# Expert second layer on one Trainium2 core: another order of its products, product 1 in two parts, expert 0's weights requested earlier

## Chip, core, metric

The kernel runs on one NeuronCore of a Trainium2 chip. The metric is the device time of one execution in microseconds (us). Before the change, three runs took 947.87 us in the median (946.37 to 949.05).

## What is computed

The input is x, 4 batches of 1024 tokens of 512 float32 values. A first, conditional linear layer picks one 512x512 matrix per batch; its result xc is routed: each token goes to the one of 8 experts with the largest router probability, at most 512 tokens an expert. Each expert is two matrix products with a ReLU between. The result, scaled with the probability, is added to x.

```python
xc = einsum('bsd,bdh->bsh', x, W[cat_ids]) + b[cat_ids][:, None, :]
probs = softmax(xc @ Wr)                      # (4096, 8)
eidx, p_tok = argmax(probs), max(probs)       # one expert a token
xe = xc[dispatch]                             # (8, 512, 512): each expert's tokens
h  = maximum(einsum('ecd,edf->ecf', xe, W1), 0.0)   # F = 2048
ye = einsum('ecf,efd->ecd', h, W2) * p_tok
y  = x + scatter_add(ye)
```

## The kernel before

All products are float32 and use a seven-product scheme for 2x2 blocks (Strassen's in Winograd's form): both factors are cut in four blocks, VectorE (DVE) forms sums of blocks, TensorE (PE) multiplies seven pairs, numbered 1 to 7, and the results are added up in PSUM banks and by DVE.

The span has two parts. The first some 146 us are the conditional layer and the routing; xc goes to DRAM in two halves of the columns (`xc0_dram`, `xc1_dram`), written by line 511. After that come the eight experts e = 0 to 7, some 98 us each.

An expert's first layer runs over NG = 4 groups g of the 2048 columns. `first_layer(e, g, k)` is product k of group g: 4 matmuls of 128x256 (line 743; the profile counts two records for each float32 matmul). ScalarE (ACT) copies banks out (L758) and applies the ReLU (L763, L770), DVE adds (L762), and after the last product of a group, number 3, `sums` (L160 to L163) forms the block sums of the group's h, which the second layer multiplies. The weights w1 come in three rotating buffers, so a load of w1 waits until PE has left the buffer.

The second layer contracts over all 2048 columns of h. `second_layer(e, k)` is product k for k in 1, 6, 5, 7: two row tiles `at` of 8 matmuls 128x256 each, 16 in all (L797). Products 1, 6 and 7 are accumulated one on top of the other in the same PSUM bank `yx`; product 5 has the bank `yy`. After each product DVE adds the bank, scaled by `table`, to the `residual` rows (`add`, L788): two adds after 1 and after 6, four after 5 and after 7. Since 6 accumulates on 1 and 7 on 6, a product must wait until the adds of the one under it have read the bank.

The other three products, 2, 4 and 3, are again cut in seven small products each: `inner_sums(e, k)` lets DVE make 8 sums (L160 to L163 on h, L167 to L170 on w2), in place over the blocks of a product that PE has finished, and `inner_product(e, k, q)` runs 4 matmuls of 128x128 (L848) and one or two adds of 128x128 (L788). The small products have the banks x (1, 6, 7, 4 on top of each other), y (5, 3) and z (2).

`transpose_rows(e + 1, c)` (L716) turns the next expert's row tiles c = 0 to 3 between the products; ACT copies them out and DVE forms their sums (L726 to L730). For e = 0, whose rows are gathered by GpSimd (POOL, L688, lines of `gather`) from `xc0_dram` and `xc1_dram`, the transposes stand between the first products, the two column halves apart.

`load_w2(e)` (L666) is four loads of 1 MB on SyncE's queue (SP), `sum_w2(e, part)` (L167 to L170, 128x1024) is DVE's block sums of half of them, `fetch(e)` gathers the residual rows and the next expert's rows, and line 899 copies x to the output in three pieces in expert 0.

The order on PE and SP is that of the program text (`manual_schedule`). On DVE, ACT and POOL a scheduler chooses it; `behind(f)` asks that f comes after the latest of the adds L762, and the adds `add` have high priority. SP works through its list in order: a load that waits holds back those after it.

Of the kernel before, what the change touches and what calls it, by code (L numbers as in the profile page):

```python
# [11 lines left out]
ALU = mybir.AluOpType  # L12
# [4 lines left out]
P = 128  # L17
# [5 lines left out]
def kernel(  # L23
# [14 lines left out]
    E, _, F = w1.shape  # L38
# [8 lines left out]
    SC = CAP // P  # L47
    HK = KC // 2
    HC = SC // 2
    HD = D // 2  # L50
# [22 lines left out]
    def behind(f, *at):  # L73

        with tc.issue_after(latest[0].ins):
            f(*at)
# [68 lines left out]
    BANK = {1: "x", 2: "z", 3: "y", 4: "x", 5: "y", 6: "x", 7: "x"}  # L145
    OPENS = (1, 2, 5)
    LAST = {"x": 4, "y": 3, "z": 2}
    banks = {}

    def bank(pool, key, k, shape, name, bufs):  # L150

        tag = BANK[k]
        if k in OPENS:
            at = "_".join(str(n) for n in key)
            banks[key, tag] = pool.tile(shape, F32, tag=tag, bufs=bufs, name=f"{name}{tag}_{at}")
        return banks[key, tag]

    def sums(eng, a11, a12, a21, a22, s1, s2, s4):

        eng.tensor_tensor(s1, a21, a22, ALU.add)  # L160
        eng.tensor_tensor(a21, a11, a21, ALU.subtract)
        eng.tensor_tensor(s2, s1, a11, ALU.subtract)  # L162
        eng.tensor_tensor(s4, a12, s2, ALU.subtract)  # L163

    def differences(eng, b11, b12, b21, b22, t1, t2, t4):

        eng.tensor_tensor(t1, b12, b11, ALU.subtract)  # L167
        eng.tensor_tensor(b12, b22, b12, ALU.subtract)
        eng.tensor_tensor(t2, b22, t1, ALU.subtract)
        eng.tensor_tensor(t4, b21, t2, ALU.subtract)  # L170

    w1s, w2s = {}, {}
# [12 lines left out]
    def sum_w1(e, g):  # L185
        sums(nc.vector, *(w1s[e, g][:, k, :, :] for k in range(7)))
# [469 lines left out]
    ps_p = ctx.enter_context(tc.tile_pool(name="ps_p", bufs=2, space=PSUM, reuse_waits="tile"))  # L656
# [3 lines left out]
    def load_w2(e):  # L660

        names = ("b11", "b12", "b21", "b22", "t1", "t2", "t4")
        t = {k: w2p.tile([P, NG * HB, D // 2], F32, tag=k, name=f"w2_{k}_{e}") for k in names}
        for k in ("b11", "b21", "b12", "b22"):
            i, j = int(k[1]) - 1, int(k[2]) - 1
            nc.sync.dma_start(  # L666
                out=t[k],
                in_=w2[
                    e, i * F // 2 : (i + 1) * F // 2, j * D // 2 : (j + 1) * D // 2
                ].rearrange("(m p) d -> p m d", p=P),  # L670
            )
        w2s[e] = t
# [64 lines left out]
    def first_layer(e, g, k):  # L737

        key = (1, e, g)
        ps = bank(ps_p, key, k, [P, HB, HC * P], "h", bufs=2)  # L740
        for j in range(HB):
            for kc in range(HK):
                nc.tensor.matmul(  # L743
                    ps[:, j, :],
                    lhsT=w1s[e, g][:, LEFT[k], kc, j * P : (j + 1) * P],
                    rhs=xes[e][:, RIGHT1[k], kc, :],
                    start=(k in OPENS and j == 0 and kc == 0),
                    stop=(k == LAST[BANK[k]] and j == HB - 1 and kc == HK - 1),
                    skip_group_check=True,
                )  # L750
        if e not in hs:
            hs[e] = hp.tile([P, NG, 7, HB, HC * P], F32, tag="h", name=f"h_{e}")
        h = hs[e][:, g, :, :, :]
        if k in (1, 6, 7):
            banks[key, k] = snap.tile(
                [P, HB, HC * P], F32, tag=f"s{k}", bufs=2, name=f"s{k}_{e}_{g}"
            )
            nc.scalar.copy(banks[key, k], ps)  # L758

        def total(into, ps, part):  # L760
            with tc.high_priority():
                latest[0] = nc.vector.tensor_tensor(into, ps, part, ALU.add)  # L762
            nc.scalar.activation(into, into, AF.Relu)  # L763

        if k == 2:
            total(h[:, 0, :, :], ps, banks.pop((key, 1)))
        if k == 7:
            total(h[:, 3, :, :], banks[key, "y"], banks.pop((key, 7)))
        if k == 4:
            nc.scalar.activation(h[:, 1, :, :], ps, AF.Relu)  # L770
        if k == 3:
            total(h[:, 2, :, :], ps, banks.pop((key, 6)))
            sums(nc.vector, *(h[:, i, :, :] for i in range(7)))
# [10 lines left out]
    def add(e, ps, half, at, columns):  # L784

        row = residual[e * SC + half * HC + at][:, columns]
        with tc.high_priority():
            nc.vector.scalar_tensor_tensor(  # L788
                row, ps, table[:, half * HC + at, e, 0:1], row, ALU.mult, ALU.add
            )  # L790

    def second_layer(e, k):

        ps = bank(ps_p, (2, e), k, [P, HC, HD], "y", bufs=2)
        for at in range(HC):
            for m in range(NG * HB):
                nc.tensor.matmul(  # L797
                    ps[:, at, :],
                    lhsT=hs[e][:, m // HB, LEFT[k], m % HB, at * P : (at + 1) * P],
                    rhs=w2s[e][RIGHT2[k]][:, m, :],  # L800
                    start=(k in OPENS and at == 0 and m == 0),
                    stop=(k in ENDS and at == HC - 1 and m == NG * HB - 1),
                    skip_group_check=True,
                )
        for half, part in {1: [(0, 0)], 6: [(0, 1)], 5: [(1, 1), (0, 1)], 7: [(1, 1), (1, 0)]}[k]:
            for at in range(HC):
                add(e, ps[:, at, :], half, at, slice(part * HD, (part + 1) * HD))
# [69 lines left out]
    def between(e, g):  # L877

        if g == 0 and e > 0:
            behind(sum_w1, e, W1G - 2)  # L880
        if g > 0:
            if e > 0 or g > 2:
                first_layer(e, g - 1, 4)
                first_layer(e, g - 1, 3)
            ahead = e * NG + g - 1 + W1G
            if ahead < E * NG:
                load_w1(*divmod(ahead, NG))
            if ahead > W1G and ahead <= E * NG:
                behind(sum_w1, *divmod(ahead - 1, NG))
        if g >= 2:  # L890
            behind(sum_w2, e, g - 2)
        if g == 1:
            behind(fetch, e)
        if e == 0 and g > 0:

            if g == 1:
                load_w2(0)
            q = slice((g - 1) * T // (NG - 1) // P * P, g * T // (NG - 1) // P * P)
            nc.sync.dma_start(out=of[q, :], in_=xf[q, :])

    with tc.manual_schedule(engines={mybir.EngineType.PE, mybir.EngineType.SP}):
        gather(0, xg, xc_dram, rows, src_row)

        for part, half, then in (
            ([0], 0, [(0, 1)]),
            ([0], 1, [(1, 1), (0, 5), (1, 5)]),
            ([1], 0, [(0, 2)]),
            ([1], 1, [(1, 2)]),
        ):
            for c in range(half * HC, (half + 1) * HC):  # L910
                transpose_rows(0, c, part)
            for g, k in then:
                first_layer(0, g, k)
        for e in range(E):
            for g in range(NG):
                if e == 0 and g < 2:

                    for k in ((6, 7), (4, 3))[g]:
                        first_layer(e, 0, k)
                        first_layer(e, 1, k)  # L920
                    between(e, g)
                    continue
                first_layer(e, g, 1)
                first_layer(e, g, 2)
                between(e, g)
                first_layer(e, g, 6)
                first_layer(e, g, 5)
                first_layer(e, g, 7)
            second_layer(e, 1)
            first_layer(e, NG - 1, 4)  # L930
            first_layer(e, NG - 1, 3)
            if (e + 1) * NG - 1 + W1G < E * NG:
                load_w1(e + 1, W1G - 1)
            inner_sums(e, 2)
            for c, k in enumerate((6, 5, 7)):
                second_layer(e, k)
                if k in (6, 5):
                    inner_sums(e, 4 if k == 6 else 3)
                if e + 1 < E:
                    transpose_rows(e + 1, c)  # L940

            TURNS = (1, 5, 2, 6, 3, 7, 4)
            for q in TURNS:
                if q == 4 and e + 1 < E:
                    transpose_rows(e + 1, SC - 1)
                inner_product(e, 2, q)
            for q in TURNS:
                inner_product(e, 3, q)
                inner_product(e, 4, q)
            if e + 1 < E:  # L950
                load_w2(e + 1)

# [30 lines left out]
```

## Time and profile before

| | |
|---|---|
| median of 3 runs | 947.87 us (946.37 to 949.05) |
| the profiled execution | 947.93 us, span 946.1 us |
| mean granted TensorE clock | 0.996 |
| PE busy | 923.4 us, 98% of the span |
| DVE busy | 617.7 us, 65% |
| ACT, POOL busy | 185.6 us and 177.9 us, 20% and 19% |
| DMA | 123.28 MB, mean 130 GB/s |

Times in the views count from the start of the span. A row of a timeline gives the start, the length, the engine, the source line, the operation, the tiles it writes and reads, the shape, the number of records and, in brackets, how long the engine was idle before it and what ended that. The modelled end of a matmul lies some 0.16 us after the start of the next one, so a gap of PE in brackets is by that much shorter than the time that its issue lost.

### The profile page before, as it was taken

The page shows a single profiled execution, that of the slowest core. Times are in us where ns is not written, and L with a number is a line of the kernel's source. Part 1 is how long each engine was busy: PE and PEld are TensorE (multiplying, and loading weights), DVE is VectorE, ACT ScalarE, POOL GpSimd, SP SyncE. Part 2 cuts the span into 40 slices and gives each one's busy share as a digit, 9 for nine tenths or more (in the row PEclk, how much of TensorE's full clock was granted, in tenths as well). Part 3 has the DMA queues.
Part 4 walks back from the last instruction along what each step waited for, and adds up shares of the span by engine and source line. Part 5 has one row for each costly group of instructions (what it writes and reads, how often), then busy time and mean ns, then how long its engine had stood idle before and what let it go on. Part 6 is the DMA issues. An engine that isn't in the chain of part 4 may idle for free.

```text
span 946.1 us, 12760 instructions
## 1 busy us (share of the span) xinstructions
PE 923.4 (98%) x5126; PEld 814.6 (86%) x5126; DVE 617.7 (65%) x1134; ACT 185.6 (20%) x317; POOL 177.9 (19%) x173
## 2 busy tenths in 40 slices
PE   9999999989999999999999999999999999999996
PEld 6788787878988898889888998899889988998886
DVE  4656673578449844985478647963797468745782
ACT  3333201310132103210330023101310132013200
POOL 0042342230141013200230024001500150012001
PEclk9999999999999999999999999999999999999999
DMA  9474223695633153314441345115520652062001
GB/s 307 158 233 155 84 91 94 211 387 202 222 116 107 45 190 128 129 45 148 137 155 45 103 163 171 54 52 171 178 89 5 216 177 89 1 219 89 0 1 45
DMA packets 95724, 123.28 MB, mean 130 GB/s; under 512 B 8516, under 2 KB 83268, under 8 KB 95474
## 3 DMA queue, kind: packets, MB, share of 16 engines
q1 hardware_dynamic: 85634, 97.54, 30.8%
q0 software_dynamic: 9216, 24.85, 8.0%
q8 instruction: 40, 0.66, 0.3%
q14 instruction: 18, 0.15, 0.1%
q10 hardware_dynamic: 816, 0.08, 0.1%
HBM read 105.96 MB, written 25.23 MB: 139 GB/s over the span
## 4 chain that ended last, share of the span: by engine, by line
PE 74%; issue 17%; DVE 4%; POOL 2%; DMA 2%; ACT 1%; SPq 1%; POOLq 0%; DVEq 0%
PE hx L743 18%; PE yx L797 11%; PE hy L743 8%; PE yx L848 7%; PE xcx_lin L488 6%; PE hz L743 4%; PE yy L797 4%; PE yy L848 3%; PE xcy_lin L488 2%; PE yz L848 2%; DMA w_b<-in_L_ffn_W_dram 2%; PE xcz_lin L488 1%; PE ps_xT L273 1%; PE ps_e L716 1%; POOL rows L688 1%
## 5 line engine op out<-in xcount | busy, mean ns | idle before, releaser
L743 PE MATMUL hx<-xe,w 128*128 128x256 f32 x1024 | 237.7, 379 | 1.2 <-DVE xe L717 1.0
L743 PEld LDWEIGHTS hx<-xe,w 128*128 128x128 f32 x1024 | 193.8, 190 | 27.7 <-DVE xe L717 1.2
L867 POOL DMA_INDIRECT out_dram<-rows,dst_row x32 | 32.0, 999 | 496.8 <-DVE rows L788 492.2
L743 PE MATMUL hy<-xe,w 128*128 128x256 f32 x512 | 120.6, 379 | 0.0
L797 PE MATMUL yx<-w_b,h 128*128 128x256 f32 x512 | 113.1, 379 | 0.0
L743 PEld LDWEIGHTS hy<-xe,w 128*128 128x128 f32 x512 | 97.3, 190 | 13.2
L797 PEld LDWEIGHTS yx<-w_b,h 128*128 128x128 f32 x512 | 96.7, 190 | 12.9
L758 ACT COPY s<-hx 128x512 f32<-128x512 f32 x96 | 55.8, 581 | 240.8 <-PE hx L743 240.8
L788 DVE SCALAR_TENSOR_TENSOR rows<-yx,table,rows 128x128 f32<-128x128 f32 (+1 forms) x160 | 60.0, 400 | 60.1 <-PE yx L848 37.1
L762 DVE TENSOR_TENSOR h<-hy,s 128x512 f32<-128x512 f32 x64 | 44.0, 688 | 74.6 <-PE hy L743 50.2
L763 ACT ACTIVATE h<-h 128x512 f32<-128x512 f32 x96 | 60.5, 630 | 159.5 <-DVE h L762 159.5
L797 PE MATMUL yx<-w_t,h 128*128 128x256 f32 x256 | 60.5, 391 | 10.6 <-DVE h L162 8.7
L688 POOL DMA_INDIRECT rows<-in_x_dram,at x32 | 41.2, 1288 | 139.6 <-DVE at L699 106.2
L797 PEld LDWEIGHTS yx<-w_t,h 128*128 128x128 f32 x256 | 49.1, 194 | 20.8 <-DVE h L162 11.9
L688 POOL DMA_INDIRECT rows<-xc_dram,at x56 | 58.6, 1047 | 17.1 <-issue 15.2
L743 PE MATMUL hz<-xe,w 128*128 128x256 f32 x256 | 60.6, 379 | 0.6 <-DVE xe L717 0.6
L762 DVE TENSOR_TENSOR h<-hz,s 128x512 f32<-128x512 f32 x32 | 22.0, 688 | 57.5 <-PE hz L743 57.5
L797 PE MATMUL yy<-w_t,h 128*128 128x256 f32 x256 | 56.6, 379 | 0.0
L743 PEld LDWEIGHTS hz<-xe,w 128*128 128x128 f32 x256 | 48.5, 190 | 7.4 <-DVE xe L717 0.9
L460 POOL DMA_INDIRECT slots<-row,dest x32 | 36.3, 1135 | 95.8 <-DVE dest L456 87.3
L797 PEld LDWEIGHTS yy<-w_t,h 128*128 128x128 f32 x256 | 48.1, 190 | 6.2
L717 ACT COPY xe<-ps_e 128x512 f32<-128x512 f32 x28 | 16.4, 586 | 182.9 <-PE ps_e L716 182.9
(154 smaller groups left out, 1258.4 us busy)
## 6 DMA issues: line engine op xcount, KB each, us to landing
w<-in_L_ffn_W_dram SPq DMA_DIRECT2D x64, 512.0 KB, 4.2
w_b<-in_L_ffn_W_dram SPq DMA_DIRECT2D x32, 1024.0 KB, 6.9
x<-in_x_dram SPq DMA_DIRECT2D x7, 1024.0 KB, 8.6
xc_dram<-s SPq DMA_DIRECT2D x22, 256.0 KB, 2.7
out_dram<-in_x_dram SPq DMA_DIRECT2D x2, 2816.0 KB, 23.9
cw<-in_L_cond_W_dram SPq DMA_DIRECT2D x3, 1024.0 KB, 9.9
out_dram<-in_x_dram SPq DMA_DIRECT2D x1, 2560.0 KB, 18.9
xc_dram<-xc SPq DMA_DIRECT2D x8, 256.0 KB, 2.3
```

Of the source, the lines that this page charges most:

```text
L460: nc.gpsimd.indirect_dma_start(out=slots, out_offset=bass.IndirectOffsetOnAxis(ap=dest[:, j : j + 1], axis=0), in_=row[:, j, :], in_offset ...
L488: nc.tensor.matmul(ps[:, j, :], lhsT=left[:, kc, j * P : (j + 1) * P], rhs=right[k][:, kc, :], start=((k in OPENS or (b, k) == (LATE, 3)) ...
L688: nc.gpsimd.indirect_dma_start(out=into[e * SC + c][:, j * n : (j + 1) * n], out_offset=None, in_=source, in_offset=bass.IndirectOffsetOnA ...
L717: (nc.vector.tensor_copy if e == 0 else nc.scalar.copy)(t[:, 2 * half + parts[0] : 2 * half + parts[0] + n, :, at * P : (at + 1) * P].rear ...
L743: nc.tensor.matmul(ps[:, j, :], lhsT=w1s[e, g][:, LEFT[k], kc, j * P : (j + 1) * P], rhs=xes[e][:, RIGHT1[k], kc, :], start=(k in OPENS an ...
L758: nc.scalar.copy(banks[key, k], ps)
L762: latest[0] = nc.vector.tensor_tensor(into, ps, part, ALU.add)
L763: nc.scalar.activation(into, into, AF.Relu)
L788: nc.vector.scalar_tensor_tensor(row, ps, table[:, half * HC + at, e, 0:1], row, ALU.mult, ALU.add)
L797: nc.tensor.matmul(ps[:, at, :], lhsT=hs[e][:, m // HB, LEFT[k], m % HB, at * P : (at + 1) * P], rhs=w2s[e][RIGHT2[k]][:, m, :], start=(k ...
L848: nc.tensor.matmul(ps, lhsT=left[:, g, :], rhs=right[:, g, :], start=(q in OPENS and g == 0), stop=(q == LAST[BANK[q]] and g == NG - 1), s ...
L867: nc.gpsimd.indirect_dma_start(out=of, out_offset=bass.IndirectOffsetOnAxis(ap=dst_row[:, n : n + 1], axis=0), in_=residual.pop(n), in_off ...
```

## The change

In words: product 1 of the second layer is issued in two halves, one row tile before the last two first-layer products (4 and 3 of group 3) and one after them; then come products 5, 6 and 7, where before it was 6, 5, 7. The sums for the small products follow their new order (product 3's after 5, product 4's after 6). The small products take other turns: number 4 of group 2 stands behind the next expert's last transpose and the first of group 3; then come pairs of 3 and 4 in another order. In `sums` and `differences` the second and third operation change places. Expert 0's w2 is requested right after the first small set of first-layer products in the program text, ahead of the load of w1 for group 3, and its sums are asked for one group earlier.

```diff
     def sums(eng, a11, a12, a21, a22, s1, s2, s4):
         eng.tensor_tensor(s1, a21, a22, ALU.add)
+        eng.tensor_tensor(s2, s1, a11, ALU.subtract)
         eng.tensor_tensor(a21, a11, a21, ALU.subtract)
-        eng.tensor_tensor(s2, s1, a11, ALU.subtract)
         eng.tensor_tensor(s4, a12, s2, ALU.subtract)
     # differences: t2 before b12, in the same way
...
-    def second_layer(e, k):
-        ps = bank(ps_p, (2, e), k, [P, HC, HD], "y", bufs=2)
-        for at in range(HC):
+    def second_layer(e, k, tiles=range(HC)):
+        if tiles[0] == 0:
+            bank(ps_p, (2, e), k, [P, HC, HD], "y", bufs=2)
+        ps = banks[(2, e), BANK[k]]
+        for at in tiles:
...
+        if tiles[-1] < HC - 1:
+            return
...
-        if g >= 2:
-            behind(sum_w2, e, g - 2)
+        part = g - 2 + (e == 0)
+        if part in (0, 1):
+            behind(sum_w2, e, part)
...
-            if g == 1:
-                load_w2(0)
...
+        behind(load_w2, 0)          # ahead of the loop over the experts
...
-            second_layer(e, 1)
+            second_layer(e, 1, [0])
             first_layer(e, NG - 1, 4)
             first_layer(e, NG - 1, 3)
+            second_layer(e, 1, [1])
...
             inner_sums(e, 2)
-            for c, k in enumerate((6, 5, 7)):
+            for c, k in enumerate((5, 6, 7)):
                 second_layer(e, k)
-                if k in (6, 5):
-                    inner_sums(e, 4 if k == 6 else 3)
+                if k in (5, 6):
+                    inner_sums(e, 3 if k == 5 else 4)
                 if e + 1 < E:
                     transpose_rows(e + 1, c)
-            TURNS = (1, 5, 2, 6, 3, 7, 4)
-            for q in TURNS:
-                if q == 4 and e + 1 < E:
-                    transpose_rows(e + 1, SC - 1)
+            for q in (1, 5, 2, 6, 3, 7):
                 inner_product(e, 2, q)
-            for q in TURNS:
-                inner_product(e, 3, q)
-                inner_product(e, 4, q)
+            if e + 1 < E:
+                transpose_rows(e + 1, SC - 1)
+            for k, q in (
+                *[(3, 1), (2, 4), (3, 5)],
+                *[(4, 1), (4, 5), (3, 2), (4, 2), (3, 6), (4, 6)],
+                *[(3, 3), (4, 3), (3, 7), (4, 7), (3, 4), (4, 4)],
+            ):
+                inner_product(e, k, q)
```

More of the change, by code (lines that the diff above doesn't have):

```diff
@@ L167, in differences @@
         eng.tensor_tensor(t1, b12, b11, ALU.subtract)
+        eng.tensor_tensor(t2, b22, t1, ALU.subtract)
         eng.tensor_tensor(b12, b22, b12, ALU.subtract)
-        eng.tensor_tensor(t2, b22, t1, ALU.subtract)
         eng.tensor_tensor(t4, b21, t2, ALU.subtract)
```

## The prediction, made before the changed kernel was run

> **What bounds the kernel.** I read the page's first part and the waits of PE first, then the timelines of one expert's second layer.
>
> ```profile
> PE 923.4 (98%) x5126; PEld 814.6 (86%) x5126; DVE 617.7 (65%) x1134; ACT 185.6 (20%) x317; POOL 177.9 (19%) x173
> ```
>
> TensorE is busy all the time and the change neither adds nor removes a matmul. So only PE's idle time, and stretches at a lower clock, can move. The list of who waited for whom, PE alone, says where they are:
>
> ```profile
> PE yx L797 <- DVE h L162: 8.7, 8, 2.4
> PE yx L797 <- DVE rows L788: 1.8, 1, 1.8
> PE yx L848 <- DVE rows L788: 0.4, 1, 0.4
> ```
>
> Once in each expert, product 6 waits for the sum L162 (s2 of the last group's h), and in expert 0 it waits before that for the adds of product 1. The PE timelines of expert 0 and expert 1:
>
> ```profile
> 204.44 1.89 PE L743 MATMUL hy<-xe,w 128*128 128x256 f32 x8
> 208.16 2.86 PE L797 MATMUL yx<-w_t,h 128*128 128x256 f32 x12 [1.83 <-DVE rows L788]
> 213.40 6.27 PE L797 MATMUL yx<-w_t,h 128*128 128x256 f32 x20 [2.38 <-DVE h L162]
> 219.51 0.60 PE L716 MATMUL ps_e<-ident,rows 128*128 128x128 f32 x4
> ...
> 309.36 2.75 PE L797 MATMUL yx<-w_t,h 128*128 128x256 f32 x12
> 313.03 4.58 PE L797 MATMUL yx<-w_t,h 128*128 128x256 f32 x20 [0.91 <-DVE h L162]
> 317.45 0.60 PE L716 MATMUL ps_e<-ident,rows 128*128 128x128 f32 x4
> 317.88 7.07 PE L797 MATMUL yy<-w_t,h 128*128 128x256 f32 x32
> ```
>
> A product of 16 matmuls takes 6.91 us when nothing waits (317.88 to the next transposes at 324.79), 0.432 us a matmul. In expert 1 product 6 is issued from 309.36 to 317.45, so 1.18 us are lost: the wait and 0.1 us of slow start. In expert 0 it could start at 206.17 and ends at 219.51, so 6.43 us are lost. The two waits don't explain that: 20 records took 6.27 us, not 4.58. The table by stretches does; the third number from the end is the granted clock, which is 1.00 in the stretches before and after:
>
> ```profile
> 214.00:218.00 4.00, 4.00 (x13) 3.21 (x11) 4.00 (x7) 0.00 (x0) 0.00 (x0) 0.57 1.15 448
> ```
>
> After 4.2 us of idleness within 7 us the clock was halved for a while, which cost 1.64 us. All eight losses add up to 6.43 + 7 x 1.18 = 14.7 us.
>
> **The new order: what goes.** Product 5 needs s1 only, and half of product 1 (3.46 us) now stands behind the last first-layer product. In expert 1's times: half of 1 at 299.00, the products 4 and 3 from 302.46 to 305.91, the other half to 309.36, then 5. The sum s1 comes at about 308.2 and is needed at 5's seventh matmul, at 311.95. So the 14.7 us go.
>
> **What comes.** Product 7 accumulates on product 6, and they are now neighbours, with only the transposes (0.43 us) between. In the changed instruction order 7's first matmul waits for the second of 6's two adds, both of which wait for 6's last matmul. Before, product 5 (6.91 us) lay between. And the adds stand in DVE's list behind all sums that the new order packs there. DVE's spacings are in its timeline of expert 1:
>
> ```profile
> 309.56 0.69 DVE L762 TENSOR_TENSOR h<-hy,s 128x512 f32<-128x512 f32 x1 [0.48 <-PE hy L743]
> 310.95 0.69 DVE L160 TENSOR_TENSOR h<-h 128x512 f32<-128x512 f32 x1 [0.69 <-ACT h L763]
> 311.68 0.69 DVE L161 TENSOR_TENSOR h<-h 128x512 f32<-128x512 f32 x1
> 312.29 0.68 DVE L162 TENSOR_TENSOR h<-h 128x512 f32<-128x512 f32 x1
> ...
> 317.83 0.87 DVE L788 SCALAR_TENSOR_TENSOR rows<-yx,table,rows 128x256 f32<-128x256 f32 x2
> 318.62 0.68 DVE L163 TENSOR_TENSOR h<-h 128x512 f32<-128x512 f32 x1
> ```
>
> L762 to L160 is 1.39 us (the ReLU between), a sum 0.60 us, 0.73 us when it needs the one before it, two adds 0.79 us, four 1.57 us. From the end of first-layer product 3 (306.09 now) the list runs without a gap: 1.39; four sums 2.53; adds of product 1 0.79; eight sums 4.82; two sums 1.21; four adds of 5 1.57; six sums 3.62; four sums 2.54; two adds of 6 with the signal 0.92. That ends at 325.48, while PE could start 7 at 324.05: 1.43 us and a slow start of 0.10. I take 1.53 us for experts 0 to 6. In expert 7 there are no transposes and the adds stand one sum earlier: 324.88 against 323.19, so 1.79 us. Sum 12.5 us. The net of this part is **-2.2 us**: expert 0 wins 4.9, the other seven lose 2.7. It holds for expert 0 because its DVE no longer lags: it stood idle for w_b's DMA 2.1 and 3.4 us there, and the w2 sums now come before 195 us.
>
> **The turns of small products.** Small product 4 of group 2 waits for the add of 7 today. Behind the transposes the issue starts 0.17 us late and loses 0.10 more, seven times; in expert 7, without transposes, 0.71 us: 2.6 us in all. The order puts (3,1), 0.89 us, between, and this goes. But (4,1) reuses the bank of (2,4), whose add ends just when (4,1) could start (2.67 against 2.68 us after the transposes, by the same rows): between 0 and 0.27 us each; I take 0.1, near a slow start alone. **-1.9 us** (-2.6 to -0.7).
>
> **Expert 0's weights.** The four loads have nothing left to wait for when SP reaches them: they follow the last write of xc, issued at 147.51 us, while before the load of w1 ahead of them held them until 174.6. At the 308 to 373 GB/s of the stretches from 176 to 190 us the 4 MB are under way for 11 to 14 us, from 148 to about 162, when POOL gathers expert 0's rows. The DMA view of 140 to 225 us shows what a gather takes from issue to landing in three conditions: expert 0's own (2.7 us for the four of the second half, which have the queues to themselves), those with copies of x in flight, and those with w2 in flight.
>
> ```profile
> rows<-xc_dram,src_row POOLq DMA_INDIRECT x8, 2.9
> rows<-xc_dram,at POOLq DMA_INDIRECT x8, 10.0
> rows<-in_x_dram,at POOLq DMA_INDIRECT x4, 6.0
> ```
>
> The second tile of the second half is issued at 151.80 and lands at 154.5; PE wants it at 155.86 and hides up to 1.36 us of delay. At 6.0 us it lands at 157.8: PE waits **+2.0 us**; the third and fourth tile are hidden by that. Bounds: nothing (gathers beside one 1 MB load of w1 had medians of 2.7 to 3.4), and 5.9 us at 10.0. The third row is the nearest: pieces of w2 in flight and hardly a copy yet. A wait of 2.0 beside the 0.63 us already there may halve the clock; 1.6 more. The Trainium skill, "DMA: Bandwidth & Descriptors" (Queues, rings and completion order), says that each DMA engine takes packets from its queues in turn. By that rule a small gather would lose only an equal share, this term would be near nothing and the sum 943.8. The Trainium skill, "TensorE: Matmul & The Clock Gate" (Part 1), ties a halved clock to an idle window of about 3.4 us; by it no wait here would halve it, though in the trace gaps of 1.83 and 2.38 us did.
>
> **What costs nothing.** The exchanged lines in `sums` bring s2 0.6 us earlier. The load of w1 for group 3 is now behind w2 on SP, but waits until 173.5 for its buffer anyway, after the queue is empty; if not, PE needs it at 183.7, five us after it landed before. The index copy for `fetch` slips some 6 us behind the w2 sums on DVE, and POOL's twelve gathers with it; expert 1's first tile, landed at about 203 before, lands at 209 and is needed at 213. The next w2 loads start about 1 us later, long before DVE wants them.
>
> **Sum.** Against the profiled 947.93 us (the median is 947.87): -2.2 - 1.9 + 2.0 gives **945.8 us**. A measurement of this kernel can tell about 0.3%, 2.8 us, from no change: faster means under 945.0, slower over 950.7.
>
> **Rivals.**
> 1. The gathers aren't delayed by more than 1.4 us: 943.8, own range 942.8 to 944.6. For it: the rows beside w1. Against: those loads were 1 MB, this stream is 4 MB. Chance 0.25.
> 2. Slower: the gathers take the 10 us of the second row, PE stands 5.9 us at 156 and restarts at half clock, 1.64: 947.93 - 4.1 + 7.6 = 951.4. It decides from about 9 us of landing. Against: that row had copies in flight. Chance 0.14, with 0.03 for halved clocks at the eight new waits (up to 13 us; the seven of 0.91 us left it whole).
> 3. The change does all it says and product 7 finds its adds done: 947.93 - 14.7 - 1.9 + 2.0 = 933.3. Against: the adds can't start before product 6 ends, and take longer than the transposes. Chance 0.05.
>
> The likeliest case has 0.53 and its own range is 944.0 to 947.6 (DVE's list 0.2 us longer or shorter in each expert, the bounds of the small products, 1 to 3.6 us for the gathers); 0.06 of it is under 945.0. Faster: 0.25 + 0.05 + 0.06 = 0.36. Slower: 0.14 + 0.03 = 0.17. The range of 8 in 10 leaves out rival 3 and the far ends of the others: 943.0 to 951.0.
>
> **What would show it.** Right: in the waits of PE, L799 on DVE h L162 is gone, and L799 on DVE rows L788 stands there eight times, with about 1.25 us each and 1.5 in expert 7; a new wait at L716 for gathered rows near 156 us; the clock stays whole at 214. Wrong: product 7 starting right behind the transposes, a wait of product 5, or gathers of 2.7 us near 150.

## The result and the profile after

The changed kernel takes 949.16 us in the median of 18 runs (947.78 to 950.89), the kernel before 946.85 in 18 runs beside it: 1.0023 times as long, 95% interval 1.0016 to 1.0030. Two later groups of runs gave 1.0010 (0.9995 to 1.0024) and 1.0017 (1.0008 to 1.0027). The forecast was 2.1 us less than before; it became some 2 us more. The profiled execution took 949.79 us, its span is 948.0.

The page's busy times, then two rows from the list of who waited for whom, PE alone (us in total, times, longest):

```profile
PE 922.8 (97%) x5126; PEld 815.7 (86%) x5126; DVE 612.6 (65%) x1134; ACT 185.5 (20%) x317; POOL 185.8 (20%) x173
```

```profile
PE yx L799 <- DVE rows L788: 10.6, 8, 1.6
PE ps_e L716 <- DMA rows<-xc_dram,src_row: 2.3, 2, 1.7
```

The row "DVE h L162" is gone. Its place is taken by eight waits at product 7, and two waits for gathered rows are new. The PE timeline of expert 1 shows one of the eight:

```profile
317.10 7.07 PE L799 MATMUL yx<-w_t,h 128*128 128x256 f32 x32
324.01 0.60 PE L716 MATMUL ps_e<-ident,rows 128*128 128x128 f32 x4
325.95 7.17 PE L799 MATMUL yx<-w_b,h 128*128 128x256 f32 x32 [1.33 <-DVE rows L788]
```

Product 7 could start 0.43 us after the transposes, at 324.44, and starts at 325.95: 1.51 us, and 0.10 more in its slow start. The start of expert 0, PE again:

```profile
153.41 3.62 PE L743 MATMUL hy<-xe,w 128*128 128x256 f32 x16
158.69 0.41 PE L716 MATMUL ps_e<-ident,rows 128*128 128x128 f32 x2 [1.66 <-DMA rows<-xc_dram,src_row]
159.74 0.41 PE L716 MATMUL ps_e<-ident,rows 128*128 128x128 f32 x2 [0.65 <-DMA rows<-xc_dram,src_row]
160.67 3.61 PE L743 MATMUL hz<-xe,w 128*128 128x256 f32 x8 [0.52 <-DVE xe L717]
```

In the profile of before, the same transposes and the same product hz follow one another without a wait for rows:

```profile
155.64 0.60 PE L716 MATMUL ps_e<-ident,rows 128*128 128x128 f32 x4
156.87 1.99 PE L743 MATMUL hz<-xe,w 128*128 128x256 f32 x8 [0.63 <-DVE xe L717]
```

That is 10.28 us after the first transposes (146.59), against 12.87 now (160.67 after 147.80). POOL had issued the two gathers that PE waits for here:

```profile
152.10 0.94 POOL L688 DMA_INDIRECT rows<-xc_dram,src_row  x1 [5.73 <-issue]
153.35 0.94 POOL L688 DMA_INDIRECT rows<-xc_dram,src_row  x1 [0.30 <-DVE xe L726]
```

They take 6.5 and 6.3 us from issue to landing, the third and fourth 5.7 and 5.6. The eight records of hz take 3.61 us; four records further on the same product of the other group takes 1.89. The table by stretches has the granted clock third from the end:

```profile
156.00:160.00 4.00, 1.69 (x9) 0.97 (x7) 0.42 (x1) 0.00 (x0) 0.79 (x1) 1.00 1.08 369
160.00:164.00 4.00, 3.48 (x10) 2.71 (x9) 0.42 (x1) 0.00 (x0) 0.00 (x0) 0.57 1.08 352
```

The clock is halved behind the waits. To place the loss I cut each profiled execution at PE's own marks: the first transposes of expert 0, its first second-layer matmul, the first matmul of expert 1 and of expert 7, the last matmul. Four profiles of before and three of the changed kernel (the later ones are among the experiments) give, in us:

| Profile | start | e0, first layer | e0, second layer | e1 to e6 | e7 |
|---|---|---|---|---|---|
| before | 146.59 | 49.22 | 58.30 | 587.61 | 96.50 |
| before_again | 146.92 | 49.95 | 54.75 | (590.42) | 96.51 |
| before_3 | 147.11 | 49.23 | 57.44 | 587.62 | 96.51 |
| before_4 | 148.07 | 49.23 | 57.82 | 587.62 | 96.51 |
| after | 147.80 | 53.41 | 53.29 | 589.12 | 96.49 |
| after_again | 146.84 | 54.75 | 53.83 | (591.67) | 96.49 |
| after_3 | 147.24 | 54.36 | 53.46 | 589.16 | 96.49 |

In brackets: profiles in which PE stood for some 0.2 to 1.6 us at a time at first-layer products, with nothing but its own issue behind it, now in one expert and now in another; 0.7 of the 49.95 is a stop too, which that profile puts down to ACT's copy (L758). The start is unchanged code and scatters by 1.5 us. The means differ by +4.8 in expert 0's first layer, -3.55 in its second, +1.5 in the six experts e1 to e6, and nothing in e7: +2.7 together, against 1.7 to 2.3 by the medians.

### The profile page after: what moved, and what is told of

Same layout as the page of the kernel before. It is cut to its first block, busy times and chain, and to the rows that moved or that the text cites. A ratio compares the mean times of both kernels' runs of the same rounds, so it can differ in the third digit from the quotient of the medians.

```text
span 948.0 us, 12759 instructions
## 1 busy us (share of the span) xinstructions
PE 922.8 (97%) x5126; PEld 815.7 (86%) x5126; DVE 612.6 (65%) x1134; ACT 185.5 (20%) x317; POOL 185.8 (20%) x173
## 4 chain that ended last, share of the span: by engine, by line
PE 44%; issue 26%; DVE 9%; POOL 3%; DMA 1%; ACT 0%; POOLq 0%; DVEq 0%
PE hx L743 16%; PE hy L743 7%; PE yx L852 6%; PE yx L799 6%; PE hz L743 4%; PE yy L852 3%; POOL rows L688 2%; DVE rows L788 2%; PE yz L852 1%; DVE h L161 1%; DVE h L160 1%; DVE h L163 1%; POOL out_dram L871 1%; DVE h L162 1%; DMA rows<-xc_dram,src_row 1%
## 5 line engine op out<-in xcount | busy, mean ns | idle before, releaser
L799 PE MATMUL yx<-w_b,h 128*128 128x256 f32 x512 | 115.3, 381 | 10.6 <-DVE rows L788 10.6
L758 ACT COPY s<-hx 128x512 f32<-128x512 f32 x96 | 55.8, 582 | 240.3 <-PE hx L743 240.3
L688 POOL DMA_INDIRECT rows<-in_x_dram,at x32 | 45.1, 1411 | 149.3 <-DVE at L699 106.3
L688 POOL DMA_INDIRECT rows<-xc_dram,at x56 | 62.6, 1119 | 20.4 <-issue 14.0
L799 PE MATMUL yx<-w_t,h 128*128 128x256 f32 x256 | 56.6, 379 | 0.0
```

The source lines that it names most:

```text
L688: nc.gpsimd.indirect_dma_start(out=into[e * SC + c][:, j * n : (j + 1) * n], out_offset=None, in_=source, in_offset=bass.IndirectOffsetOnA ...
L799: nc.tensor.matmul(ps[:, at, :], lhsT=hs[e][:, m // HB, LEFT[k], m % HB, at * P : (at + 1) * P], rhs=w2s[e][RIGHT2[k]][:, m, :], start=(k ...
```

## The experiments

Theory A: what the change does to the order behaves as forecast, and the loss against the forecast is expert 0's start, where the w2 loads delay the gathers. Rival B: the new order itself is the loss. Each kernel was timed beside the kernel before on the same chip; where the medians of two groups of runs differ, only the ratios to before are compared.

**1. Gathers first.**

```diff
+    landed = dram.tile([P, 1], F32, name="landed")
...
+        nc.sync.dma_start(out=landed, in_=rows[SC - 1][:, D - 1 : D])
         behind(load_w2, 0)
```

> The changed kernel, with a 512-byte copy of the last gathered row tile of expert 0 ahead of its w2 loads on SP, so that these four loads start only when all eight gathers have landed (some 156 us instead of 149). Theory A (the loss against the forecast sits in expert 0's start: the w2 loads delay the gathers, 4.2 us between the first transposes and product hy at 171.6 in the trace of before): this kernel is 4.2 us faster than the changed one, about 945.0 us, and some 2 us faster than before; no wait of PE at L716 for gathered rows, clock whole at 157 to 165 us, and the eight waits at product 7 stay. Rival B (the new order of products, not the loads, is the loss): within 1 us of the changed kernel, about 949. Rival C (the later loads bring back expert 0's waits for w2 sums at 208 to 218 us): some 945 + up to 5 = 950.

Measured: 945.09 us, 0.9965 of before (0.9952 to 0.9979); 49.22 us in expert 0's first layer. The time is A's 945.0. By the ratios to before (0.9965 against 1.0023) it is 5.5 us less than the changed kernel's, more than the 4.2 that A took from one profile; the three profiles of the changed kernel lie 4.2 to 5.5 us above 49.22, 4.95 in the mean. So the loss at the start goes, whole. The two kernels' answers on transfers (median us from issue to landing), the changed kernel's row first:

```profile
rows<-xc_dram,src_row POOLq DMA_INDIRECT x6, 5.6
```

```profile
rows<-xc_dram,src_row POOLq DMA_INDIRECT x5, 2.7
...
landed<-rows SPq DMA_DIRECT2D x1, 0.5 KB, 7.8
```

And PE has neither the wait nor the halved clock:

```profile
156.35 0.60 PE L717 MATMUL ps_e<-ident,rows 128*128 128x128 f32 x4
157.58 1.99 PE L744 MATMUL hz<-xe,w 128*128 128x256 f32 x8 [0.63 <-DVE xe L718]
```

**2. The early load alone**, old order and turns (`behind(load_w2, 0)` and the sums one group earlier, in the kernel before).

> The kernel before with only the earlier request for expert 0's w2 and the earlier sums of it; old order of products, old turns, old sums. Theory A: expert 0's start loses the 4.2 us, and expert 0's product 6 loses 1.2 instead of 6.4 us since DVE no longer waits for w2 there: 946.9 + 4.2 - 5.2 = 945.9 us, with PE waits at L716 near 157 us and half clock after them. Rival B (the order is the loss, the early load is free): 946.9 - 5.2 = 941.7. Rival C (the early load costs more than the start shows): over 948.

Measured: 947.80 us, 0.9999 of before (0.9989 to 1.0008). Its profiled execution took 945.35: 51.76 us in expert 0's first layer, with waits of 1.52 and 0.75 us but no halved clock, and 53.04 in the second. By the ratio A's 945.9 (0.9990 of its 946.9) lies just inside the interval, and B's 941.7 far outside. The profiled execution was the fastest of the eleven (the others 946.80 to 948.42); that the others lose more at the start, with a halved clock, is likely but not shown. By the median, what the load gives and takes in expert 0 cancels.

**3. The old load with the new order.**

```diff
-        part = g - 2 + (e == 0)
-        if part in (0, 1):
-            behind(sum_w2, e, part)
+        if g >= 2:
+            behind(sum_w2, e, g - 2)
...
+            if g == 1:
+                load_w2(0)
...
-        behind(load_w2, 0)
```

> The changed kernel with the request for expert 0's w2 and the sums of it in their old places; new order and turns kept. Theory A: expert 0's start wins its 4.2 us back, and expert 0's second layer loses some 3.5 us more at product 7 than now, because DVE's list there is late by the waits for w2 (2.1 and 3.4 us in before): 949.2 - 4.2 + 3.5 = 948.5, between 946.5 and 950. Rival B (the order is the loss): 949 or more, without a gain at 147 to 177 us. The clue is the stage times: first transposes to hy 25.05 us (A) or 29.2 (B).

Measured: 951.22 us, 1.0035 (1.0023 to 1.0048), above A's 946.5 to 950 and in B's 949 or more. But the start is whole (49.22), as A says, and the second layer of expert 0 takes 59.19 us, more than in any profile of before. PE's timeline:

```profile
203.98 1.99 PE L743 MATMUL hy<-xe,w 128*128 128x256 f32 x8 [1.89 <-DVE h L762]
...
227.68 4.57 PE L799 MATMUL yx<-w_b,h 128*128 128x256 f32 x13 [3.57 <-DVE rows L788]
```

DVE's list is late, since a sum of w2 stands in it that waits for its load:

```profile
196.89 1.23 DVE L168 TENSOR_TENSOR w_t<-w_b,w_t 128x1024 f32<-128x1024 f32 x1 [2.50 <-DMA w_b<-in_L_ffn_W_dram]
```

I had foreseen the second wait and not the first. So the forecast's "expert 0 wins 4.9" is not a gain of the new order at all: it comes with the early load, which has it with the old order too (53.04 in run 2).

**4. Small products between 6 and 7.**

```diff
                 if e + 1 < E:
                     transpose_rows(e + 1, c)
+                if k == 6:
+                    for q in (1, 5, 2):
+                        inner_product(e, 2, q)
-            for q in (1, 5, 2, 6, 3, 7):
+            for q in (6, 3, 7):
                 inner_product(e, 2, q)
```

> The changed kernel with three small products of group 2 (numbers 1, 5 and 2, 2.7 us) moved between product 6 and product 7, so that 7's wait for 6's adds (1.6 us an expert, 1.86 in expert 7, 1.3 in expert 0) is covered. Theory A: 12.3 us faster than the changed kernel, 936.9 us; L799 on DVE rows L788 is gone from PE's waits. Rival B (DVE's list is the bound and the wait only moves to the small products or to the next group): between 945 and 949, with new waits at L852.

Measured: 936.67 us, 0.9875 (0.9860 to 0.9891). The time is A's 936.9; by the ratios it is 14.0 us less than the changed kernel's, by the stages of the profiles 11.7, where A has 12.3. An expert takes 96.65 us where the changed kernel takes 98.19, and PE has no wait at product 7. Expert 1 on PE, with no gap left:

```profile
323.31 1.06 PE L852 MATMUL yx<-w_b,h 128*128 128x128 f32 x8
324.20 1.06 PE L852 MATMUL yy<-w_b,h 128*128 128x128 f32 x8
325.10 1.06 PE L852 MATMUL yz<-w_b,h 128*128 128x128 f32 x8
325.99 7.07 PE L799 MATMUL yx<-w_b,h 128*128 128x256 f32 x32
```

**5. Both edits.**

> Both edits of the two earlier runs in one kernel: expert 0's w2 loads held until its gathers have landed, and small products 1, 5 and 2 of group 2 between product 6 and product 7. Theory A (two separate losses that add up): 945.1 - 12.4 = 932.7 us, with no wait of PE at product 7 and none for gathered rows near 157 us; up to 0.9 us may stay as a wait for expert 1's first rows near 215 us. Rival (the small products only covered because PE was late by the gathers): 935 or more.

Measured: 934.85 us, 0.9853 (0.9826 to 0.9880), beside a before of 949.52 on that chip: 14.7 us less, where A's sum is 14.2 less than before (946.9 to 932.7). The sum of the two measured ratios would be 0.9817, the repeat in run 12 has 0.9840: they add up within the noise. In the trace expert 0's first layer takes 49.22 us as in run 1, and an expert without other stops 96.7 as in run 4.

**6. The old order with the load mended** (run 1's edit in run 2's kernel).

> The kernel before (old order, old turns) with expert 0's w2 requested early, behind its gathers, and summed one group earlier. It is the partner of gathers_first with the old order. Theory A (5.2 us of expert 0's loss at product 6 go with the early load alone, and the new order with its turns is itself a net loss of about 1.1 us: 6.0 + 7 x 1.59 in place of 8 x 1.17 + 2.6 small): 945.1 - 1.1 = 944.0, or by before's profile 947.9 - 5.2 + up to 0.9 (rows of expert 1 later) = 943.6. Rival (the new order is a gain once expert 0's start is mended): over 946.

Measured: 944.50 us, 0.9951 (0.9934 to 0.9967). Its interval and that of run 1 (0.9965) overlap, so the times alone don't order the two. In the traces one expert takes 97.98 us from product 6 to the next product 6, against 98.19 from product 7 to product 7 in run 1: with its turns, the new order costs about 0.2 us in each of e1 to e6 and gains nothing in e7. B is true to that small extent: the order, taken by itself, is no gain.

**7. The old turns in the changed kernel.**

```diff
-            for q in (1, 5, 2, 6, 3, 7):
+            for q in TURNS:
+                if q == 4 and e + 1 < E:
+                    transpose_rows(e + 1, SC - 1)
                 inner_product(e, 2, q)
...
+            for q in TURNS:
+                inner_product(e, 3, q)
+                inner_product(e, 4, q)
```

> The changed kernel with the old turns of the small products (group 2 whole with the transposes ahead of its number 4, then 3 and 4 in pairs). Theory A (the new turns gain 1.9 us, 0.27 less 0.1 in seven experts and 0.71 in the last): 949.2 + 1.9 = 951.1 us, with PE waits at L852 on L788 back in expert 7 (0.44 us). Rival (the turns are hidden or lose): 949.2 or less.

Measured: 952.87 us, 1.0039 (1.0023 to 1.0056), which overlaps the changed kernel's 1.0023. In the traces one expert takes 98.42 us where the changed kernel takes 98.18, and e7 takes 97.20 for 96.49: 7 x 0.24 + 0.71 = 2.4 us. The turns gain, a little more than the 1.9 forecast.

**8. The kernel before, again.**

> The kernel before, profiled once more. It is to tell how much one profiled execution differs from another. In the first profile expert 0's second layer ran at half clock near 214 us and its first transposes stood at 146.59 us; that of the changed kernel had them at 147.80. Theory A (the start and the halved clock vary from execution to execution): the first transposes at 146.6 to 147.8, and expert 0's second layer, first product to the next expert's first, 58.3 us with a halved clock or 56.7 without. Rival (the start is a property of the changed program): 146.6 again.

> The kernel before, profiled a third time: what does expert 0 lose at product 6? The first profile shows 6.43 us (a wait for the adds of product 1, the wait for the sum, a halved clock), the second 2.7 us (the wait for the sum alone). Theory A (6.43 us is the bad end of a scatter from execution to execution, so that the forecast's gain of 4.9 us was too large by up to 3.6 us): between 2.7 and 6.5 us, and with the fourth profile a mean of the four under 5. Rival (6.4 us is the rule): 6 or more in both.

> The kernel before, profiled a fourth time; the theories expect of it what they expect of before_3: between 2.7 and 6.5 us lost at expert 0's product 6 (A), or 6 and more (rival).

Measured: 949.93 us beside 949.52, and single executions of 947.59 and 948.95. The table above has the stages. Expert 0's second layer without any loss is 58.30 - 6.43 = 51.87 us, so the four profiles lose 6.43, 2.88, 5.57 and 5.95 us at product 6. PE in before_again and in before_4:

```profile
207.35 2.86 PE L797 MATMUL yx<-w_t,h 128*128 128x256 f32 x12
212.60 4.58 PE L797 MATMUL yx<-w_t,h 128*128 128x256 f32 x20 [2.38 <-DVE h L162]
```

```profile
209.37 2.86 PE L797 MATMUL yx<-w_t,h 128*128 128x256 f32 x12 [1.55 <-DVE rows L788]
214.62 6.07 PE L797 MATMUL yx<-w_t,h 128*128 128x256 f32 x20 [2.39 <-DVE h L162]
```

With only the second wait, 20 records take 4.58 us; with both, 6.07 and 6.27. Neither forecast comes out: the mean is 5.2 and not under 5, as A wanted, and the two new ones are 5.57 and 5.95, not 6 or more. The first profile is the highest of the four, but three of them lie close together and only one is low.

**9. The changed kernel, again.**

> The changed kernel, profiled once more, beside before_again. Theory A: the waits for gathered rows near 158 us are there again (1.4 to 1.7 and 0.65 to 1.1 us), followed or not by some us at half clock; the eight waits at product 7 are within 0.05 us of the first profile; first transposes between 146.6 and 147.8 us. Rival (the waits for rows were chance): none of them.

> The changed kernel, profiled a third time, beside filled_wait. Expected: waits for gathered rows of 2.0 to 2.7 us in all, hz at half clock in two executions of three, the eight waits at product 7 as before (10.3 us), 1.5 to 2.5 us slower than before.

Measured: 952.10 us beside 950.38 and 949.36 beside 947.27. The waits for rows were 2.19 + 0.51 and 1.38 + 1.01 us, with hz at 3.78 us both times: what the first profile shows came in all three.

**10. Only half of the load early** (b11 and b21 ahead of the gathers, the copy `landed` and b12 and b22 behind them).

> The changed kernel with only two of expert 0's four w2 loads ahead of its gathers (2 MB), the other two after the gathers have landed. Theory A (the gathers are slow as long as the 4 MB stream: it lasts from 149 to 166 us in the changed kernel): the stream is over at about 156 us, PE waits 0.3 to 1.0 us in all for gathered rows instead of 2.3, the clock stays whole, about 3 us faster than the changed kernel, 946 us where that has 949. Rival (each gather pays a fixed price as soon as any load is in flight): the waits of 1.7 and 0.65 us stay, 949.

Measured: 950.84 us, 1.0002 (0.9989 to 1.0016), beside after_again's 952.10: 1.3 us where A expected 3, and not told apart from it. The page of transfers shows these loads over at about 156 us, as expected, but PE still waits:

```profile
156.66 0.41 PE L720 MATMUL ps_e<-ident,rows 128*128 128x128 f32 x2 [1.53 <-DMA rows<-xc_dram,src_row]
157.39 0.41 PE L720 MATMUL ps_e<-ident,rows 128*128 128x128 f32 x2 [0.33 <-DMA rows<-xc_dram,src_row]
158.31 3.60 PE L747 MATMUL hz<-xe,w 128*128 128x256 f32 x8 [0.52 <-DVE xe L721]
```

That listing's start is 145.90 us: 10.8 us after it the first tile is there, against 10.9, 11.4 and 10.6 in the changed kernel's three profiles; the second tile is there after 11.5 us, against 11.9 to 12.3. Half the bytes don't bring the first tile sooner, and the second by less than 1 us. A's picture (a delay that shrinks with the stream) fails for the first tile; here 2 MB in flight were enough.

**11. The wait filled with idle matmuls.**

```diff
+            if (part, half) == ([1], 0):
+                keep_warm(ps_e, 3)
             for c in range(half * HC, (half + 1) * HC):
                 transpose_rows(0, c, part)
```

> The changed kernel with three idle matmuls of 128x512 (0.85 us each, 2.56 us; their result is not used) on PE ahead of expert 0's transpose of the second column half, where PE now waits 1.4 to 2.2 us and then 0.5 to 1.1 us for gathered rows. Theory A (PE's idleness there halves the clock behind it): product hz behind the wait runs whole, 1.9 to 2.0 us for 8 records instead of 2.8 to 3.8, so 1 to 1.7 us faster than the changed kernel on the same chip, less up to 0.3 us by which the idle matmuls outlast the wait. Rival (the clock is halved by the load of the DMA queues or by the step in work, not by the idleness): hz at half clock again and no gain.

Measured: 947.71 us beside after_3's 949.36 on the same chip, ratio to before 1.0007 (0.9998 to 1.0016); its 11 runs lie between 947.14 and 948.11, those of the changed kernel between 947.41 and 950.38. PE:

```profile
155.98 2.74 PE L69 MATMUL ps_idle<-idle 128*128 128x512 f32 x6
158.55 0.74 PE L716 MATMUL ps_e<-ident,rows 128*128 128x128 f32 x4
159.81 1.99 PE L743 MATMUL hz<-xe,w 128*128 128x256 f32 x8 [0.52 <-DVE xe L717]
```

hz starts 12.89 us after the first transposes, about as late as in the changed kernel (12.87 to 13.51), but runs whole, and expert 0's first layer takes 51.83 us. The stream of loads is the same, so it was PE's idleness that halved the clock; by the medians the halving is 1.65 us of the changed kernel's time.

**12. The fetch ahead of the w2 sums**, in the kernel of run 5, and that kernel once more beside it.

```diff
+        if g == 1:
+            behind(fetch, e)
         part = g - 2 + (e == 0)
         if part in (0, 1):
             behind(sum_w2, e, part)
-        if g == 1:
-            behind(fetch, e)
```

> both_mended with fetch(0) asked for ahead of the w2 sums, so that the index copy and with it POOL's gathers of expert 1's rows come before DVE's wait for w2. Theory A (PE's wait of 0.8 to 1.0 us at expert 1's first rows near 215 us comes from the index copy behind the w2 sums): that wait goes, 1.0 us faster than both_mended. Rival (the rows are late because of the stream of copies and weights, not of the index copy): the wait stays and the time is that of both_mended.

> The kernel both_mended once more, beside fetch_first, so that the two are compared on one chip. Expected 1.0 us slower than fetch_first, and 1.3 to 1.6% faster than before.

Measured: 935.67 and 935.83 us, 0.9833 (0.9811 to 0.9855) and 0.9840 (0.9817 to 0.9863). The times don't tell them apart. The traces do for the wait: in PE's list both_mended_2 has

```profile
PE ps_e L717 <- DMA rows<-xc_dram,at: 1.5, 1, 1.5
```

and fetch_first has no such row; expert 0's second layer takes 51.75 us instead of 53.51. This kernel, some 1.6% faster than before, has the lowest ratio of the runs, though the times don't tell it from run 5's.

## Why the prediction was wrong, step by step

- **Expert 0's weights: the term that failed most.** Forecast +2.0, measured +4.8 in the mean of the profiles. The mechanism was right: the w2 loads delay the gathers and PE waits. Two things in the term were sized wrong. The first is the wait: hz starts 2.6, 3.2 and 2.9 us later after the first transposes than in before, not 2.0. POOL issued the second tile's gather 5.6 to 6.5 us after these transposes, where before had 5.2, and the first two gathers took 6.5 and 6.3 us in the first profile, not the 6.0 of the sum (which is the middle of the four). The second is the clock, which the text has as "may halve the clock; 1.6 more" and left out of the sum: it halved in all three profiles and cost another 1.6 to 2.3 us there, 1.65 by the medians of run 11. It belonged into the likeliest case: 1.83 and 2.38 us of idleness had halved it in before.
  How much idleness it takes, these runs don't settle. Gaps of 1.38, 1.01 and 0.52 us within 4 us halved the clock, and 1.53, 0.33 and 0.52 us (2.38 in all) did so in run 10; 1.52, 0.75 and 0.52 us (2.79 in all) did not in run 2, nor did one gap of 2.38 us in before_again. The Trainium skill, "TensorE: Matmul & The Clock Gate" (Part 1), speaks of an idle window of some 3.4 us; no gap here is that long, so the trace decides against reading the rule as one gap. The page also calls the window free-running, which would fit with the different outcomes, but no run here shows the window.
  Beside the loads the four gathers took 5.6 to 6.5 us instead of 2.7, with half of the loads PE starts on the first two 6.3 and 5.8 us after their issue, and a copy of 512 bytes, issued 0.4 us ahead of the loads, took 7.8 us to land (what it takes alone no run shows). The Trainium skill, "DMA: Bandwidth & Descriptors" (Queues, rings and completion order), has each DMA engine take packets from its queues in turn; the delay near nothing that the forecast worked out from this is not what the trace shows.
- **The gain at product 6: read from one execution.** The 14.7 us were right for the profile at hand (the clock's part in them is 6.27 - 4.58 = 1.69 us, not 1.64), and the waits are gone. But 6.43 of them were expert 0's, in the highest of four profiles, which have 5.2 in the mean. With 1.4 to 2.0 us lost there now, expert 0's second layer gains 3.55 us, not 5.1 (4.9 and 0.2 of the turns).
- **Product 7's new wait: right.** 1.53 forecast and 1.59 measured (1.49 and 0.10 of slow start), 1.79 and 1.86 in expert 7; only expert 0, where PE comes later, has less (0.96 to 1.32). The packed list of DVE, added up row by row, gave this almost to the digit, and run 4 shows that an expert wins 1.3 us against before (96.65 for 97.94) once the wait is filled.
- **The turns: right**, 2.4 us instead of 1.9.
- **"What costs nothing": wrong in one point.** The index copy for `fetch` behind the w2 sums made expert 1's rows late: 0.27, 1.11 and 0.73 us in the three profiles of the changed kernel, up to 1.7 in those with the load mended. Run 12 moves the copy and the wait is gone. I had allowed for a slip of 6 us and for gathers as quick as before. POOL began them 9.9 us later (44.7 against 34.7 us after the first transposes), and beside copies of x and loads of w1 the gathers of the residual rows took some 12 us each, not 6.0.

Expert 0's start is 2.8 us worse than forecast, its second layer 1.5 us, e1 to e6 0.4 us and e7 0.1: together 4.8, which turns -2.1 into the +2.7 of the profiles. Of the rivals the second came nearest in kind: a shorter wait than its 5.9 us, with the clock halved, 4.8 us in all and not 7.6. What stays open is why a gather beside large loads takes 3 us more, whether they are 2 or 4 MB.

## What to carry to other kernels

A load that has nothing left to wait for starts beside whatever is in flight at that moment: before asking for it sooner, find the small transfers on the critical path there, and let it start behind them. When one product must not follow another directly because its bank is still being read, put independent work between the two; exchanging the order only moved the wait here (1.18 us an expert before, 1.59 after). Take a loss that you mean to remove from more than one execution, and if a step adds idleness to TensorE, put the halved clock into the sum.

## What the hardware showed beyond that

Some 2.4 to 3.2 us of idleness, in pieces, cost another 1.3 to 2.3 us at half clock, in six of the seven profiles in which PE waited for rows behind the early loads: the changed kernel scatters over 3 us from run to run, and over 1 us once idle matmuls fill the gap. An idle matmul in front of a known wait can pay for itself.
